# A four-stage network kernel on one core: the finishing of the first attention pinned to its order on VectorE, the norms' shifts gathered into one addition, and pools that wait tile by tile

## The chip, the cores and the metric

The kernel runs on one core of a Trainium2 chip. The metric is the device time of one execution in microseconds. Engines are called PE (TensorE, the matrix unit; PEld is its weight load), DVE (VectorE), ACT (ScalarE), POOL (GpSimd) and SP (SyncE, which issues the transfers). Each engine works through its own list of instructions in order and waits at an instruction until what it needs has been signalled.

## The reference, cut to what matters

All in fp32, T = 1024 tokens of D = 256. Four blocks stand one behind the other, each with a norm before and a norm behind it:

```
x = x + layernorm(attention(layernorm(x)))      # L0: 16 heads of 16, rope, softmax, + its own input
x = x + layernorm(experts_L0(layernorm(x)))     # 8 experts, F = 256, two with low-rank parts
x = x + layernorm(recurrent(layernorm(x)))      # L1: conv over 4 tokens, 16 heads of 128, gated
x = x + layernorm(experts_L1(layernorm(x)))     # 16 experts of 176, the top 4, and a shared one of 352

def layernorm(x):                               # over the 256 values of a token, eps = 1e-5
    m = mean(x); v = var(x)
    return (x - m) / sqrt(v + eps)
```

For the change one property counts: a layernorm does not see a number that is added to all 256 values of a token. The second norm's part in x, written out, is x + acc·rs − mean·rs, where acc is the block's output and rs is 1/sqrt(var + eps). The last term is one number per token.

## The kernel before, in words

The 1024 tokens are 8 tiles of 128 (TT = 8), worked on as four pairs. `x`, `acc` (a block's output) and `hT` (the normed x, channels first, the input of the next block's matmuls) stay in SBUF for the whole run. The four blocks are methods called one after the other: `attention0`, `experts0`, `attention1`, `experts1`. Each opens its own pools of SBUF and PSUM buffers (`a_...`, `b_...`, `c_...`, `d_...`); a block's pools take the memory that the block before it gave back. Weights come by transfers on SP's queue, some groups ahead of use.

**Order.** The program is traced in Python, and a scheduler then puts each engine's instructions in an order of its own choice, from their dependencies and the order of tracing. So two independent instructions of one engine may change places. The engines then run these lists.

**Between two blocks, `turn_over` (L248).** For each pair of tiles: DVE takes the statistics of both `acc` (st, mv: L180, L181), adds eps (ve, L183), POOL raises to the power of −0.5 (rs, L184), DVE works out nb = −mean·rs (L185), adds acc·rs to x (L257), takes statistics of x the same way, ACT writes h = x·rs2 + nb2 (L263), and POOL adds the first norm's nb to x (L267, the shift). Then, some steps later, `turn` (L237) lets PE transpose h (pt, L243) and ACT copy it to hT (L244). The delay is made with the list `todo`: `turn_over` puts two empty steps and the turn on it, and the gate matmuls of the next block pop steps from it (`catch_up`). At the end, `turn_out` (L279) uses the same `scales` and sends x out.

**attention0.** Two halves of 512 queries by four groups of four heads are eight steps. `largest` (L432ff) works ahead: PE scores (L448) by DVE maxima over keys (L453, 256 of them), whose negation goes into an extra row of q and k (L468, then `turned`/`signed`: transposes L406, copies L407). `attend` (L491ff) follows behind it: scores (L517), exponentials on ACT (L546), sums by PE over a block of keys (po, L504), copy of the result (oT, L509). Both are generators that are advanced alternately. When `largest` is through, `attend` takes another branch (`alone`, L526ff), with the exponentials at L535, all four scores first and then the sums of the step before.

The first half of the queries (tiles 0 to 3, two pairs) is finished while the second half is still worked on: `finished_slowly` (L555ff) is a generator, advanced by one step per score pair in `attention0`'s last loop (`next(after, None)`, L696). For each pair it transposes oT (L581), divides by the sums (rec, cx: L586, L587), transposes back (L594, L596), multiplies by w_out (L601), adds the block's own input (acc, L605), and goes through `turn_over_slowly` (L191), the same chain as `turn_over` cut into steps (L201 st, L202 mv, L206 ve, L207 rs, L208 nb, L221 x, L228 h, L233 the shift). The second half (tiles 4 to 7, the third and fourth pair) is finished by `finished(1)`, whose steps go on `todo` and are popped between the first gate matmuls of `experts0`, with `turn_over` at its end.

**The experts.** `experts` (L795ff) runs over groups of experts: gates pg and pu on PE (L765), Silu on ACT (L767), product on DVE (mid, L768), then `down` (po on PE, L783, added to acc by DVE at L791). The gates of groups 0 and 1 come first, and among them the router's logits (pl, L745). `experts1` is `experts` with `join` set. `attention1` projects (px, L1049), does the convolution's taps on DVE (y, L1041), and gates with og (L1265).

Of the kernel before, what the change touches and what calls it, by code (L numbers as in the profile page):

```python
# [15 lines left out]
P = 128  # L16
T = 1024
TT = T // P
# [31 lines left out]
class Net:  # L50
    def __init__(self, ctx, tc, a, out):
# [26 lines left out]
        self.mv0 = self.const.tile([P, TT, 2], F32, name="mv0")  # L78
        self.rs0 = self.const.tile([P, TT], F32, name="rs0")
# [8 lines left out]
        with tc.tile_pool(name="late", bufs=1) as late:  # L88
            self.w_out = late.tile([P, KC, D], F32, name="w_out")
            self.oT = late.tile([P, H * SLOT // P, T], F32, name="oT")  # L90
            with tc.tile_pool(name="awts", bufs=1) as aw:
# [99 lines left out]
    def turn_over_slowly(self, ps, tp, acc):  # L191

        nc = self.nc
# [5 lines left out]
        def stats(mv, i, src):  # L199
            st = self.small.tile([P, 6], F32, tag="st", name="st")  # L200
            nc.vector.bn_stats(st, src)  # L201
            nc.vector.bn_aggr(mv[:, i, :], st)  # L202

        def scale(mv):
            ve, rs, nb = small("ve"), small("rs"), small("nb")
            nc.vector.tensor_scalar(ve, mv[:, :, 1], EPS, None, ALU.add)  # L206
            nc.gpsimd.tensor_tensor(rs, ve, self.nhalf[:, 0:2], ALU.pow)  # L207
            nc.vector.scalar_tensor_tensor(nb, mv[:, :, 0], -1.0, rs, ALU.mult, ALU.mult)  # L208
            return rs, nb

        mv = small("mv", 2)
        for i in range(2):
            acc(i)
            yield
            stats(mv, i, accs[i])
            yield
        rs, nb = scale(mv)
        yield
        mv = small("mv", 2)
        for i, x in enumerate(xs):  # L220
            nc.vector.scalar_tensor_tensor(x, accs[i], rs[:, i : i + 1], x, ALU.mult, ALU.add)  # L221
            yield
            stats(mv, i, x)
            yield
        rs2, nb2 = scale(mv)
        h = self.row.tile([P, 2, D], F32, tag="h2", name="h")
        for i, x in enumerate(xs):
            nc.scalar.activation(  # L228
                h[:, i, :], x, AF.Identity, scale=rs2[:, i : i + 1], bias=nb2[:, i : i + 1]
            )  # L230
            yield
        for i, x in enumerate(xs):
            nc.gpsimd.tensor_scalar(x, x, nb[:, i : i + 1], None, ALU.add)  # L233
        self.turn(ps, h, tp)
        yield

# [11 lines left out]
    def turn_over(self, ps, tts):  # L248

        nc = self.nc
        tp = tts[0] // 2
        xs = self.pair(self.x, tp)
        rs, nb = self.scales(self.pair(self.acc, tp))
        for i, x in enumerate(xs):
            nc.vector.scalar_tensor_tensor(  # L257
                x, self.acc[:, 2 * tp + i, :], rs[:, i : i + 1], x, ALU.mult, ALU.add
            )
        rs2, nb2 = self.scales(xs)  # L260
        h = self.row.tile([P, 2, D], F32, tag="h2", name="h")
        for i, x in enumerate(xs):
            nc.scalar.activation(  # L263
                h[:, i, :], x, AF.Identity, scale=rs2[:, i : i + 1], bias=nb2[:, i : i + 1]
            )
        for i, x in enumerate(xs):
            nc.gpsimd.tensor_scalar(x, x, nb[:, i : i + 1], None, ALU.add)  # L267

        self.todo.extend([None, None, lambda ps: self.turn(ps, h, tp)])
# [107 lines left out]
    def attention0(self):  # L377
# [4 lines left out]
        with ExitStack() as ctx:  # L382
            big = ctx.enter_context(tc.tile_pool(name="a_big", bufs=1))
            qkp = ctx.enter_context(tc.tile_pool(name="a_qk", bufs=2))
            pp = ctx.enter_context(tc.tile_pool(name="a_p", bufs=6))
            ps = ctx.enter_context(tc.tile_pool(name="a_ps", bufs=7, space=PSUM))
            pso = ctx.enter_context(tc.tile_pool(name="a_pso", bufs=1, space=PSUM))
# [167 lines left out]
            def finished_slowly():  # L555
# [3 lines left out]
                for tp in range(QT // 2):  # L559
# [14 lines left out]
                    for _ in self.turn_over_slowly(ps, tp, acc):  # L574
# [3 lines left out]
            def by_token(tt, dst, ps):  # L578
# [7 lines left out]
                nc.vector.reciprocal(rec, pt[:, :, DH : DH + 1])  # L586
                nc.vector.tensor_tensor(dst, pt[:, :, 0:DH], rec.to_broadcast([P, H, DH]), ALU.mult)  # L587
# [11 lines left out]
            def projected(tt, cT, po):  # L599
                for k in range(KC):  # L600
# [4 lines left out]
                nc.vector.scalar_tensor_tensor(  # L605
                    self.acc[:, tt, :], self.x[:, tt, :], self.rs0[:, tt : tt + 1], po,
                    ALU.mult, ALU.add,
# [76 lines left out]
            after = iter(())  # L684
            for n, (qh, g) in enumerate(steps):
                if n == NG:
                    after = finished_slowly()
                then = None
                for inside in attend(qh, g, lambda: pulled == count):
# [3 lines left out]
                    if then:  # L693
                        then()
                        then = None
                    next(after, None)  # L696
            gather(len(sums))
# [97 lines left out]
    def experts(self, ps, tmp, midp, groups, route, weigh, then, join=False):  # L795
# [62 lines left out]
        for g in range(2, len(groups)):  # L858
            tiles = groups[g]()
            for hf in range(2):  # L860
# [21 lines left out]
    def experts0(self):  # L882
        nc, tc, a = self.nc, self.tc, self.a
        with ExitStack() as ctx:
            one = ctx.enter_context(tc.tile_pool(name="b_one", bufs=1))
            midp = ctx.enter_context(tc.tile_pool(name="b_mid", bufs=4))
            tmp = ctx.enter_context(tc.tile_pool(name="b_tmp", bufs=3))
            wp = ctx.enter_context(tc.tile_pool(name="b_w", bufs=4))
            ps = ctx.enter_context(tc.tile_pool(name="b_ps", bufs=8, space=PSUM))
# [83 lines left out]
    def attention1(self):  # L973
# [3 lines left out]
        with ExitStack() as ctx:  # L977
            one = ctx.enter_context(tc.tile_pool(name="c_one", bufs=1))
            sp = ctx.enter_context(tc.tile_pool(name="c_st", bufs=9))
            ps = ctx.enter_context(tc.tile_pool(name="c_ps", bufs=4, space=PSUM))  # L980
            ps2 = ctx.enter_context(tc.tile_pool(name="c_ps2", bufs=2, space=PSUM))
# [458 lines left out]
```

## Time and profile before

| | |
|---|---|
| runs of the kernel | 1282.84, 1286.2, 1287.16 us; median 1286.2 |
| the profiled execution | 1286.36 us, of which its span (first to last instruction) 1284.6 us |
| mean granted clock of TensorE | 0.986 |
| DVE score maxima, L453 | 256 of 685 ns, 163.4 us |
| DVE statistics, L180 | 28 in 11.1 us, 414 ns each |
| POOL power, L184 | 25 in 17.5 us, 701 ns each |
| POOL shift, L267 / L233 | 20 of 968 ns / 4 of 929 ns |
| attention0, experts0, attention1, experts1 begin at | 0, 304.8, 489, 1010 us of the span |

The granted clock is the share of full speed that the chip allowed TensorE; a value of 0.50 means that matmuls take twice as long. In a timeline, a row gives start and duration in us, engine, line and operation, output <- inputs with their sizes, how many instructions were put together (x), and in brackets how long the engine had been idle before it and what ended that.

### The profile page before, as it was taken

To read this page: it belongs to the slowest core of one execution; us is meant where nothing else is said; L and a number is where in the kernel's file an instruction comes from. 1 tells how busy PE (TensorE), PEld (TensorE's weight loads), DVE (VectorE), ACT (ScalarE), POOL (GpSimd) and SP (SyncE) were. 2 spreads that over 40 slices of the span, in tenths; PEclk is the share of its full clock that TensorE was granted. 3 is DMA by queue.
4 is the path that set the end of the run, shared out by engine and by line. 5 is a ranking of instruction groups with operands and counts; after the bars stand their busy time and mean duration, and the time that the engine had idled before them with its cause. 6 is when DMAs were issued, how large, how long until landed. Compare 5 with 4: busy or idle time off the path is not lost. (4 is left out here: it accounts for less than half of the span.)

```text
span 1284.6 us, 15784 instructions
## 1 busy us (share of the span) xinstructions
PE 1217.4 (95%) x6128; PEld 722.3 (56%) x6128; DVE 732.4 (57%) x1656; ACT 495.7 (39%) x912; POOL 149.3 (12%) x137
## 2 busy tenths in 40 slices
PE   7999999989999997899999999999998799999997
PEld 4533333323556564567676667767676346555655
DVE  5876767641542345776777776758675523333334
ACT  4266665655411113544544454453543221111011
POOL 3100001010200022121111112121212400000001
PEclk9999999999999998999999999999999899999999
DMA  6000000000033012002021202020210105523000
GB/s 194 1 1 1 1 1 1 1 1 1 2 129 102 0 42 83 29 33 88 23 103 34 74 33 74 34 74 33 74 41 27 62 1 158 163 82 124 20 25 33
DMA packets 38923, 64.42 MB, mean 50 GB/s; under 512 B 4776, under 2 KB 28552, under 8 KB 38848
## 3 DMA queue, kind: packets, MB, share of 16 engines
q1 hardware_dynamic: 38848, 63.41, 15.4%
q8 instruction: 48, 0.79, 0.3%
q14 instruction: 27, 0.22, 0.1%
HBM read 62.12 MB, written 1.28 MB: 49 GB/s over the span
## 5 line engine op out<-in xcount | busy, mean ns | idle before, releaser
L453 DVE TENSOR_REDUCE pm<-sc 128x1 f32<-128x512 f32 x256 | 163.4, 685 | 66.1 <-PE sc L517 42.9
L768 DVE TENSOR_TENSOR mid<-sg,pu 128x512 f32<-128x512 f32 (+1 forms) x82 | 56.4, 688 | 192.7 <-PE pu L765 163.4
L517 PE MATMUL sc<-qTm,kT 32*128 32x512 f32 x512 | 152.5, 654 | 1.2 <-DVE pm L453 1.2
L767 ACT ACTIVATE sg<-pg 128x512 f32<-128x512 f32 (+1 forms) x82 | 48.9, 596 | 270.5 <-PE pg L765 270.4
L546 ACT ACTIVATE pe<-sc 128x512 f32<-128x512 f32 x216 | 117.8, 595 | 71.0 <-PE sc L517 48.8
L448 PE MATMUL sc<-kT,qT 32*128 32x512 f32 x512 | 139.1, 645 | 1.6 <-ACT qT L407 0.8
L1089 ACT ACTIVATE sn<-pt,shift,rs 128x128 f32<-128x128 f32 x256 | 93.6, 470 | 107.2 <-DVE shift L1085 107.0
L1049 PE MATMUL px<-hT,w_l1a 128*128 128x512 f32 x256 | 124.0, 596 | 4.3 <-issue 3.5
L1041 DVE SCALAR_TENSOR_TENSOR y<-px,cp,y 128x1023 f32<-128x1023 f32 (+5 forms) x102 | 123.2, 1211 | 2.5 <-ACT y L1035 2.5
L791 DVE TENSOR_TENSOR acc<-acc,po 128x512 f32<-128x512 f32 (+1 forms) x61 | 41.1, 674 | 100.1 <-PE po L783 100.1
L765 PE MATMUL pg<-hT,w_l1f 128*128 128x512 f32 (+1 forms) x200 | 97.1, 609 | 0.7 <-ACT hT L244 0.7
L765 PE MATMUL pu<-hT,w_l1f 128*128 128x512 f32 (+1 forms) x200 | 94.7, 596 | 0.0
L783 PE MATMUL po<-w_l1f,mid 128*128 128x256 f32 (+1 forms) x400 | 87.5, 379 | 0.0
L1084 POOL TENSOR_TENSOR rs<-ve,nhalf 128x8 f32<-128x8 f32 x32 | 52.4, 1638 | 299.8 <-DVE ve L1083 245.1
L504 PE MATMUL po<-pe,va 128*32 128x256 f32 (+1 forms) x872 | 80.9, 440 | 4.0 <-ACT oT L509 3.3
L783 PEld LDWEIGHTS po<-w_l1f,mid 128*128 128x128 f32 (+1 forms) x400 | 76.0, 190 | 13.4 <-issue 3.3
L517 PEld LDWEIGHTS sc<-qTm,kT 32*128 32x128 f32 x512 | 49.7, 187 | 53.7 <-issue 41.9
L184 POOL TENSOR_TENSOR rs<-ve,nhalf 128x2 f32<-128x2 f32 (+1 forms) x25 | 17.5, 701 | 464.2 <-DVE ve L183 459.7
L1183 PE MATMUL pg<-hT,w_l1a 128*128 128x512 f32 x128 | 61.9, 609 | 6.9 <-DVE og L1265 5.5
L504 PEld LDWEIGHTS po<-pe,va 128*32 128x32 f32 x872 | 17.8, 108 | 89.0 <-issue 77.5
L765 PEld LDWEIGHTS pu<-hT,w_l1f 128*128 128x128 f32 (+1 forms) x200 | 38.5, 192 | 49.5 <-issue 49.5
L765 PEld LDWEIGHTS pg<-hT,w_l1f 128*128 128x128 f32 (+1 forms) x200 | 38.1, 192 | 44.9 <-issue 43.5
(205 smaller groups left out, 1932.6 us busy)
## 6 DMA issues: line engine op xcount, KB each, us to landing
spread<-rows SPq DMA_DIRECT2D x32, 512.0 KB, 4.5
w<-w SPq DMA_DIRECT2D x16, 512.0 KB, 4.9
w_l1f<-in_e_gT SPq DMA_DIRECT2D x4, 640.0 KB, 4.0
w_l1f<-in_e_uT SPq DMA_DIRECT2D x4, 640.0 KB, 5.3
w_l1f<-in_e_dT SPq DMA_DIRECT2D x4, 640.0 KB, 8.0
w_l0f<-in_e_wg SPq DMA_DIRECT2D x4, 512.0 KB, 5.0
w_l0f<-in_e_wu SPq DMA_DIRECT2D x4, 512.0 KB, 6.5
w_l0f<-in_e_wd SPq DMA_DIRECT2D x4, 512.0 KB, 7.4
```

The lines of the kernel that those rows point to most:

```text
L448: nc.tensor.matmul(sc, raw[r, tt * P : (tt + 1) * P], kT[r, g, half(kh)], start=True, stop=True,)
L453: nc.vector.tensor_reduce(pm[:, tt, 2 * pair + i, kh : kh + 1], sc, AX.X, ALU.max)
L504: nc.tensor.matmul(po[0][rows(j), c], va[:, st, g * G + j, :], pe[j // 2][:, j % 2, c], start=(st == 0), stop=(st == TT - 1 and c.stop == ...
L517: nc.tensor.matmul(sc, kT[rows(j), g, st * P : (st + 1) * P], qm[rows(j), :], start=True, stop=True,)
L546: nc.scalar.activation(pe[pair][:, i, :], sc, AF.Exp, scale=scale)
L765: nc.tensor.matmul(p, w(k), self.hT[:, k, c], start=(k == 0), stop=(k == KC - 1))
L768: nc.vector.tensor_tensor(mid, sg, pu, ALU.mult)
L783: nc.tensor.matmul(po[:, i, :], left[:, at * P : (at + 1) * P], right, start=(n == 0), stop=(n == len(pieces) - 1),)
L1041: nc.vector.scalar_tensor_tensor(y[:, at:hi], px[:, at - j : hi - j], column(cw + 4 * h + 3 - j), y[:, at:hi], ALU.mult, ALU.add,)
L1049: nc.tensor.matmul(px[:, c], w[:, k, hh * DK : (hh + 1) * DK], self.hT[:, k, c], start=(k == 0), stop=(k == KC - 1),)
L1089: nc.scalar.activation(sn[:, n, :], pts[n // 4][:, n % 4, :], AF.Identity, scale=rs[:, n : n + 1], bias=shift[:, n : n + 1],)
L1183: nc.tensor.matmul(pg, wg[:, k, hh * DK : (hh + 1) * DK], self.hT[:, k, c], start=(k == 0), stop=(k == KC - 1),)
```

## The change

Three things are altered.

1. `turning` takes the place of `turn_over_slowly` and of the body of `turn_over`. Its DVE instructions, and `rec`, `cx` and `acc` of attention0, are *pinned*: the scheduler keeps each of them on DVE behind all that was pinned before it. The second statistics are interleaved (x, st, mv of the first tile, then of the second). The steps of the finishing are advanced twice per score pair once `largest` is through, and the last transposes of q and k are put off by two steps (`late`). `turn_over` takes 12 pieces of `turning` at once and leaves the turn on `todo`, as before.
2. The POOL additions of nb to x (L233, L267) are gone. Means and rs of the first norms are kept for all eight tiles and the three blocks (`mvs`, `rss`), and `shifted`, called at the fourth group of `experts1` (g = 3), works out the sum of the three shifts on POOL and adds it to x with eight ACT instructions. nb is now worked out for the second norm only.
3. All pools of the four blocks are opened with `reuse_waits="tile"`: a buffer waits for the last users of the very bytes that it takes over, where before it waited for all users of the pool that had the memory.

The diff, cut to its core (the pools' lines all alike):

```diff
-        with tc.tile_pool(name="late", bufs=1) as late:
+        with tc.tile_pool(name="late", reuse_waits="tile", bufs=1) as late:
...
         self.nhalf = self.const.tile([P, TT], F32, name="nhalf")
         nc.gpsimd.memset(self.nhalf, -0.5)
         self.mv0 = self.const.tile([P, TT, 2], F32, name="mv0")
+        self.mvs = self.const.tile([P, 3, TT, 2], F32, name="mvs")
+        self.rss = self.const.tile([P, 3, TT], F32, name="rss")
+        self.norms = [0] * (TT // 2)
         self.rs0 = self.const.tile([P, TT], F32, name="rs0")
...
     def pair(self, v, tp):
         return [v[:, 2 * tp + i, :] for i in range(2)]
-    def turn_over_slowly(self, ps, tp, acc):
-        nc = self.nc
+    def pinned(self, ins):
+        return self.tc.keep_in_program_order(ins)
+    def turning(self, ps, tp, acc=None):
+        nc, pinned = self.nc, self.pinned
         xs, accs = self.pair(self.x, tp), self.pair(self.acc, tp)
         def small(tag, *shape):
...
         def stats(mv, i, src):
             st = self.small.tile([P, 6], F32, tag="st", name="st")
-            nc.vector.bn_stats(st, src)
-            nc.vector.bn_aggr(mv[:, i, :], st)
-        def scale(mv):
-            ve, rs, nb = small("ve"), small("rs"), small("nb")
-            nc.vector.tensor_scalar(ve, mv[:, :, 1], EPS, None, ALU.add)
+            pinned(nc.vector.bn_stats(st, src))
+            pinned(nc.vector.bn_aggr(mv[:, i, :], st))
+        def scale(mv, rs):
+            ve = small("ve")
+            pinned(nc.vector.tensor_scalar(ve, mv[:, :, 1], EPS, None, ALU.add))
             nc.gpsimd.tensor_tensor(rs, ve, self.nhalf[:, 0:2], ALU.pow)
-            nc.vector.scalar_tensor_tensor(nb, mv[:, :, 0], -1.0, rs, ALU.mult, ALU.mult)
-            return rs, nb
-        mv = small("mv", 2)
+        n = self.norms[tp]
+        self.norms[tp] += 1
+        mv, rs = (v[:, n, 2 * tp : 2 * tp + 2] for v in (self.mvs, self.rss))
         for i in range(2):
-            acc(i)
+            if acc is not None:
+                acc(i)
             yield
             stats(mv, i, accs[i])
             yield
-        rs, nb = scale(mv)
+        scale(mv, rs)
         yield
-        mv = small("mv", 2)
+        mv2, rs2 = small("mv", 2), small("rs")
         for i, x in enumerate(xs):
-            nc.vector.scalar_tensor_tensor(x, accs[i], rs[:, i : i + 1], x, ALU.mult, ALU.add)
+            pinned(nc.vector.scalar_tensor_tensor(x, accs[i], rs[:, i : i + 1], x, ALU.mult, ALU.add))
             yield
-            stats(mv, i, x)
+            stats(mv2, i, x)
             yield
-        rs2, nb2 = scale(mv)
+        scale(mv2, rs2)
+        yield
+        nb = small("nb")
+        pinned(nc.vector.scalar_tensor_tensor(nb, mv2[:, :, 0], -1.0, rs2, ALU.mult, ALU.mult))
+        yield
         h = self.row.tile([P, 2, D], F32, tag="h2", name="h")
         for i, x in enumerate(xs):
             nc.scalar.activation(
-                h[:, i, :], x, AF.Identity, scale=rs2[:, i : i + 1], bias=nb2[:, i : i + 1]
+                h[:, i, :], x, AF.Identity, scale=rs2[:, i : i + 1], bias=nb[:, i : i + 1]
             )
-            yield
-        for i, x in enumerate(xs):
-            nc.gpsimd.tensor_scalar(x, x, nb[:, i : i + 1], None, ALU.add)
+        ps = (yield) or ps
         self.turn(ps, h, tp)
         yield
+    PIECES = 12
     def turn(self, ps, h, tp):
...
     def turn_over(self, ps, tts):
-        nc = self.nc
-        tp = tts[0] // 2
-        xs = self.pair(self.x, tp)
-        rs, nb = self.scales(self.pair(self.acc, tp))
-        for i, x in enumerate(xs):
-            nc.vector.scalar_tensor_tensor(
-                x, self.acc[:, 2 * tp + i, :], rs[:, i : i + 1], x, ALU.mult, ALU.add
-            )
-        rs2, nb2 = self.scales(xs)
-        h = self.row.tile([P, 2, D], F32, tag="h2", name="h")
-        for i, x in enumerate(xs):
-            nc.scalar.activation(
-                h[:, i, :], x, AF.Identity, scale=rs2[:, i : i + 1], bias=nb2[:, i : i + 1]
-            )
-        for i, x in enumerate(xs):
-            nc.gpsimd.tensor_scalar(x, x, nb[:, i : i + 1], None, ALU.add)
-        self.todo.extend([None, None, lambda ps: self.turn(ps, h, tp)])
+        t = self.turning(ps, tts[0] // 2)
+        for _ in range(self.PIECES):
+            next(t)
+        self.todo.extend([None, None, lambda ps: t.send(ps)])
+    def shifted(self):
+        nc = self.nc
+        lost = self.small.tile([P, 3, TT], F32, tag="lost", bufs=1, name="lost")
+        shift = self.small.tile([P, TT], F32, tag="shift", bufs=1, name="shift")
+        nc.gpsimd.tensor_tensor(lost, self.mvs[:, :, :, 0], self.rss, ALU.mult)
+        nc.gpsimd.tensor_tensor(shift, lost[:, 0, :], lost[:, 1, :], ALU.add)
+        nc.gpsimd.tensor_tensor(shift, shift, lost[:, 2, :], ALU.add)
+        nc.gpsimd.tensor_scalar(shift, shift, -1.0, None, ALU.mult)
+        for tt in range(TT):
+            x = self.x[:, tt, :]
+            self.pinned(nc.scalar.activation(x, x, AF.Identity, bias=shift[:, tt : tt + 1]))
     def catch_up(self, ps, n):
...
                         po = ps.tile([P, D], F32, tag="b1", name="po")
                         projected(2 * tp + i, cT[:, :, i, :], po)
-                    for _ in self.turn_over_slowly(ps, tp, acc):
+                    for _ in self.turning(ps, tp, acc):
                         yield
                         yield
...
                         oT[:, g, tt * P : (tt + 1) * P], self.ident,
                     )
                 rec = self.small.tile([P, H, 1], F32, tag="rec", name="rec")
-                nc.vector.reciprocal(rec, pt[:, :, DH : DH + 1])
-                nc.vector.tensor_tensor(dst, pt[:, :, 0:DH], rec.to_broadcast([P, H, DH]), ALU.mult)
+                self.pinned(nc.vector.reciprocal(rec, pt[:, :, DH : DH + 1]))
+                self.pinned(
+                    nc.vector.tensor_tensor(dst, pt[:, :, 0:DH], rec.to_broadcast([P, H, DH]), ALU.mult)
+                )
             def by_channel(cx, ps):
                 cx = cx.rearrange("p i h c -> p i (h c)")
...
                         po, cT[:, k, :], self.w_out[:, k, :], start=(k == 0), stop=(k == KC - 1)
                     )
-                nc.vector.scalar_tensor_tensor(
-                    self.acc[:, tt, :], self.x[:, tt, :], self.rs0[:, tt : tt + 1], po,
-                    ALU.mult, ALU.add,
+                self.pinned(
+                    nc.vector.scalar_tensor_tensor(
+                        self.acc[:, tt, :], self.x[:, tt, :], self.rs0[:, tt : tt + 1], po,
+                        ALU.mult, ALU.add,
+                    )
                 )
             def finished(qh):
...
                 then = pull()
                 if then:
                     then()
-            after = iter(())
+            after, then, late = iter(()), None, 2
             for n, (qh, g) in enumerate(steps):
                 if n == NG:
                     after = finished_slowly()
-                then = None
                 for inside in attend(qh, g, lambda: pulled == count):
                     if inside:
                         then = pull()
                         continue
-                    if then:
+                    if pulled == count and late > 0:
+                        late -= 1
+                    elif then:
                         then()
                         then = None
                     next(after, None)
+                    if pulled == count:
+                        next(after, None)
             gather(len(sums))
             for _ in after:
                 pass
...
         behind = []
         for g in range(2, len(groups)):
             tiles = groups[g]()
+            if join and g == 3:
+                self.shifted()
             for hf in range(2):
                 half = start(g, tiles, hf)
                 if join and g >= len(groups) - 2 and (g, hf) != (len(groups) - 2, 0):
```

## The prediction

> **What bounds the kernel now.** I read the page's first part, then the idle time ahead of TensorE (PE), then the timeline at each idle place, then the granted clock around it.
>
> ```profile
> span 1284.6 us, 15784 instructions
> PE 1217.4 (95%) x6128; PEld 722.3 (56%) x6128; DVE 732.4 (57%) x1656; ACT 495.7 (39%) x912; POOL 149.3 (12%) x137
> PEclk9999999999999998999999999999999899999999
> ```
>
> PE is busy 1217.4 of 1284.6 us, so everything else can give back at most 67 us. DVE (57%) and POOL (12%) count only where PE stands still for them. PE's order is almost untouched by the change (it issues the same matmuls; the order differs only while attention0 finishes and experts0 starts), so the forecast is a sum over the few places where PE stands. They all lie where one stage is finished by norms and the next begins.
>
> ```profile
> 219.81 0.16 DVE L208 SCALAR_TENSOR_TENSOR nb<-mv,rs 128x2 f32<-128x2 f32 x1 [0.81 <-POOL rs L207]
> 220.01 1.09 ACT L228 ACTIVATE h<-x,nb,rs 128x256 f32<-128x256 f32 x2 [3.27 <-DVE nb L208]
> 220.63 1.12 PE L517 MATMUL sc<-qTm,kT 32*128 32x512 f32 x2 [1.21 <-DVE pm L453]
> 220.71 1.83 POOL L233 TENSOR_SCALAR x<-x,nb 128x256 f32<-128x256 f32 x2 [0.93 <-ACT h L228]
> ...
> 225.82 1.94 PE L504 MATMUL po<-pe,va 128*32 128x512 f32 x8
> ...
> 229.30 0.64 PE L504 MATMUL po<-pe,va 128*32 128x256 f32 x8
> ```
>
> That is the timeline where the first pair of attention0 is finished. The finishing's twelve small DVE operations came bunched between 213.9 and 220.0, the score maxima (L453) came late, PE waited 1.21 us, and then the same eight sums (L504) that take 0.64 us elsewhere took 1.94. The stretches of the clock say why:
>
> ```profile
> 218.61:222.02 3.41, 2.20 (x16) 1.03 (x14) 2.56 (x7) 2.01 (x5) 2.01 (x3) 1.00 0.00 0
> 222.02:228.85 6.83, 6.83 (x29) 2.59 (x26) 3.11 (x5) 3.19 (x7) 0.52 (x1) 0.50 0.00 0
> ...
> 476.00:479.70 3.70, 1.23 (x7) 0.53 (x5) 2.75 (x10) 0.68 (x2) 1.30 (x2) 1.00 0.00 0
> 479.70:486.50 6.80, 6.74 (x33) 5.79 (x34) 2.44 (x7) 1.46 (x3) 2.66 (x3) 1.00 0.00 0
> ```
>
> Columns: window, PE, PEld, DVE, ACT and POOL busy, granted clock. After some stalls PE runs at 0.50 for 6.83 us, which costs half of that, 3.4 us, if PE has work throughout.
>
> **The change, part by part.** Five places; times are of the profiled execution.
>
> *First pair of attention0 (215 to 230), DVE's order pinned, two sums of scores between any two pieces.* A steady group (eight score matmuls and eight sums) takes PE 1.64 to 1.66 us, by the starts of the groups away from any stall, and DVE 1.29 (two maxima of 0.65). From 214.93 to 229.87 PE did five groups, 14.94 us, against 5 x 1.64 = 8.2: 6.8 lost. Pinned, one piece (at most x 0.48 or st 0.43 + mv 0.18) falls to every two groups: 4 x 0.65 + 0.61 = 3.2 us of DVE against 3.3 of PE. It just fits, so no bunch, no stall, no slow clock. The ends are 0 (maxima late anyhow) and 6.8; I take **-6**, near the upper end, since nothing else feeds the bunch.
>
> *Second pair, tail of attention0 (268 to 305).* PE's 1.43-us wait at 270.3 for the turn of the last q and k goes (that turn is now put off by two steps).
>
> ```profile
> 283.69 0.60 ACT L228 ACTIVATE h<-x,nb,rs 128x256 f32<-128x256 f32 x1 [2.07 <-DVE nb L208]
> 284.20 0.56 ACT L509 COPY oT<-po 128x512 f32<-128x512 f32 x1
> 284.82 1.94 PE L504 MATMUL po<-pe,va 128*32 128x512 f32 x8 [3.27 <-ACT oT L509]
> ```
>
> Before, ACT waited for nb, and the copy oT behind it held PE 3.3 us; 6.83 us of half clock followed. In the new order the two h still stand ahead of that copy on ACT. nb is worked out at 280.9 (from the projection's start, now 274.0, by the old chain of 6.2 us plus 0.45 for the norm's new interleaving), so a stall like the old one stays, but from then on ACT has 28 exponentials of 0.52 us and ends near 299.7; the first gate matmul starts near 301 with no slow clock, 303.5 with it, against 304.76. Gain 1.3 to 3.9, taken **-2.2**.
>
> *Start of experts0 (321 to 340), third and fourth pair.* This is what the change costs.
>
> ```profile
> 330.56 1.09 ACT L263 ACTIVATE h<-x,nb,rs 128x256 f32<-128x256 f32 x2 [3.36 <-DVE nb L185]
> ...
> 334.77 1.09 ACT L263 ACTIVATE h<-x,nb,rs 128x256 f32<-128x256 f32 x2 [2.64 <-DVE nb L185]
> 335.42 0.93 PE L243 MATMUL pt<-ident,h 128*128 128x128 f32 x4
> ...
> 339.62 3.63 PE L745 MATMUL pl<-wr,hT 128*128 128x8 f32 x32
> ```
>
> Before, the scheduler mixed the two pairs: the sums acc of all four tiles stood ahead of the third pair's x, and the fourth pair's nb came 4.2 us after the third's. Pinned, the fourth pair's acc (tile 6) stands behind the third pair's nb on DVE (331.3). Behind it wait PE's projection of tile 7 (same PSUM bank; PE gets there near 330, so 1.3 to 1.9 us idle), then acc 7, and the whole chain: st, idr's copy (0.66), st, mid (0.69), ve, pow 0.73, x, st, x, st, mid, ve, pow, nb = 9.3 us from 331.8, nb near 341, first h near 340.5 to 341.7. PE reaches the fourth pair's transposes near 337 and waits 3.7. The router's logits, 339.62 before, come near 344.5 to 345.5: **+5**. Ends: 0 (DVE fills the waits for pow with mids, and all pairs come 1 us earlier) and +8 with half clock. A stall of 3.3 us (284.82, above) and one of 3.5 (498.88, below) each stood beside 6.83 us at 0.50, one of 2.47 at 477 did not; so I add 0.6 x 3.4 = **+2**.
>
> *experts0 to attention1, attention1 to experts1 (470 to 512, 991 to 1015).* All turns now go x, st, mv, x, st, mv, which costs 0.45 us against x, x, st, st, mv, mv (each mv waits for its st). Where PE already waits for h, this is paid: 2.47 us at 477 becomes about 3, +0.5, or +3.9 if the clock falls there; I take **+0.5** and **+1** for a third of a chance.
>
> ```profile
> 498.88 1.18 PE L243 MATMUL pt<-ident,h 128*128 128x128 f32 x4 [3.48 <-ACT h L263]
> ...
> 1001.73 0.93 POOL L267 TENSOR_SCALAR x<-x,nb 128x256 f32<-128x256 f32 x1 [0.93 <-ACT h L263]
> 1002.63 0.73 POOL L184 TENSOR_TENSOR rs<-ve,nhalf 128x2 f32<-128x2 f32 x1
> 1008.25 1.18 PE L243 MATMUL pt<-ident,h 128*128 128x128 f32 x4 [5.63 <-ACT h L263]
> ```
>
> Here POOL's x (0.93) does stand ahead of a pow that the chain waits for; its removal gives 0.75 to 0.9, the interleaving and one convolution tap (0.7) that now precedes the norm's last ve take it back: **0** at 499. At 1002 the first pair's nb comes about 2 us later and the last h about 0.6: **+0.6** (-0.5 to +1.5).
>
> *The shifts.* 24 POOL adds of 0.93 to 0.97 us (22.9 us) go; POOL is 12% busy and, but for the two places above, nobody waits for them: 0. The new ones are four small POOL operations and eight ACT operations 128x256, like h (0.55): 4.4 us in experts1, where ACT has one Silu of 0.6 us per 3.44 us of PE. PE has eight banks ahead of it: 0, at worst 1. They would have to delay a Silu by more than those banks hold to be seen. If that cover were gone, it would be the 4.4 us. The pools' finer waits change one place I can find: the first px (489.27, idle 1.76) need not wait for the last acc, 1.8 us earlier, but the next transposes wait for h at 498.9 either way: 0.
>
> Sum: -6 - 2.2 + 5 + 2 + 0.5 + 1 + 0.6 = **+0.9**. From the profiled 1286.36 (span 1284.6 and 1.8 around it; the median 1286.2 is the same) that gives **1287**. A difference under 0.3% (3.9 us) can't be told from none.
>
> [...]
>
> **Rivals.**
>
> *Faster, about 1279* (1275 to 1282.4). The fourth pair's norm isn't late: the new stalls at 330 and 337 are short because PE's start moves 2 us ahead and DVE's mids fall elsewhere; then -6 - 2.2 + 1 = -7. For it: DVE has idle time around 329 to 336. Against: acc 6 is behind nb in the built order.
>
> *Slower, about 1293* (1290.2 to 1297). One mechanism: the fourth pair's acc behind the third's nb at the start of experts0, stall 3.7 + 1.9, the half clock in full after it (+3.4), and no gain from the tail: -6 + 5.6 + 3.4 + 0.5 + 3.4 (the same at 477) = +7. It decides as soon as the first pair gains less than the fourth loses. For it: 3.5 us idle at 495 did bring the half clock.
>
> *Nothing of it works*: DVE's pinned pieces still bunch (3.2 of 3.3 us leaves no slack), first pair's slow clock stays: -2 + 8 = 1292; this lies in the same range as the slower rival.
>
> **How the numbers follow.** Forecast 0.41 (own range 1282.5 to 1290.1), faster 0.29, slower 0.25, nothing works 0.05. The range 1277.5 to 1295 reaches into both sides and leaves out the ends of each. Faster by over 0.3% 0.29, within 0.41, slower 0.30.
>
> **What would show it.** Right: no PE row of over 1 us of idle and no clock of 0.50 between 214 and 232; the transposes of the fourth pair with an idle of 3 us or more for h, and logits 4 us or more after the first gate plus 34.9 (before: 339.62 - 304.76); px 2 us earlier with the same end. Wrong: a half clock at 222 still there; logits within 36 us of the first gate; the tail's stall gone (a copy oT ahead of h on ACT); a Silu of experts1's group 3 with PE idle behind it.

## The result, and the profile after

The changed kernel takes 1285.95 us (median of 12 runs, 1284.49 to 1290.56) against 1285.98 (12 runs, 1282.84 to 1287.38): ratio 1.0005, interval 0.9995 to 1.0015. No difference can be told. The profiled execution took 1284.57 us with a span of 1282.5, 1.8 less than that of before.

That is not because nothing happened. The first lines of the page after, for the sum, and the clock of the stretch where the first pair of attention0 is finished (window, PE, PEld, DVE, ACT and POOL busy, granted clock):

```profile
span 1282.5 us, 15734 instructions
PE 1215.0 (95%) x6128; PEld 722.3 (56%) x6128; DVE 733.5 (57%) x1644; ACT 498.6 (39%) x920; POOL 126.9 (10%) x117
```

```profile
215.20:222.02 6.82, 6.82 (x56) 2.30 (x48) 5.39 (x11) 4.63 (x9) 0.71 (x1) 1.00 0.00 0
222.02:228.85 6.83, 6.83 (x68) 2.50 (x64) 5.86 (x11) 4.34 (x8) 0.00 (x0) 1.00 0.01 2
```

PE does 68 matmuls from 222.02 to 228.85 where it did 29, at full clock. Then, in the timeline of the kernel after, the tail of attention0, and the first gate of experts0:

```profile
274.60 0.16 DVE L239 SCALAR_TENSOR_TENSOR nb<-mv,rs 128x2 f32<-128x2 f32 x1 [0.81 <-POOL rs L216]
274.80 1.09 ACT L243 ACTIVATE h<-x,nb,rs 128x256 f32<-128x256 f32 x2 [2.42 <-DVE nb L239]
...
276.42 1.12 PE L529 MATMUL sc<-qTm,kT 32*128 32x512 f32 x2 [1.86 <-ACT pe L547]
277.70 0.60 ACT L521 COPY oT<-po 128x512 f32<-128x512 f32 x1
...
296.41 1.99 PE L784 MATMUL pg<-hT,w_l0f 128*128 128x512 f32 x4
```

ACT still waits 2.42 us for nb with its two h ahead of the exponentials, and PE waits for these. And the start of experts0:

```profile
321.92 0.16 DVE L239 SCALAR_TENSOR_TENSOR nb<-mv,rs 128x2 f32<-128x2 f32 x1 [0.81 <-POOL rs L216]
322.00 0.47 DVE L620 SCALAR_TENSOR_TENSOR acc<-x,rs,po 128x256 f32<-128x256 f32 x1
...
322.53 1.13 PE L615 MATMUL po<-w_out,cT 128*128 128x256 f32 x4 [0.90 <-DVE acc L620]
...
331.08 1.09 ACT L243 ACTIVATE h<-x,nb,rs 128x256 f32<-128x256 f32 x2 [3.71 <-DVE nb L239]
331.74 0.44 PE L258 MATMUL pt<-ident,h 128*128 128x128 f32 x2 [3.35 <-ACT h L243]
...
337.36 3.63 PE L764 MATMUL pl<-wr,hT 128*128 128x8 f32 x32
```

The fourth pair's acc runs right behind the third pair's nb (322.00 after 321.92), the projection of tile 7 waits for it (0.90), and 9 us later the transposes wait 3.35 us for its h. The logits stand 40.95 us behind the first gate (296.41). In the kernel before it was 34.86, from its logits at 339.62 and its first gate:

```profile
304.76 1.98 PE L765 MATMUL pg<-hT,w_l0f 128*128 128x512 f32 x4 [0.68 <-ACT hT L244]
```

The later turns, in the timeline of the same kernel: the first projection px no longer waits, the last pair's transposes wait longer, and at the end of attention1 two pairs are waited for instead of one.

```profile
477.56 0.93 PE L258 MATMUL pt<-ident,h 128*128 128x128 f32 x4 [2.63 <-ACT h L243]
...
485.24 1.88 PE L1070 MATMUL px<-hT,w_l1a 128*128 128x512 f32 x4
...
496.30 1.18 PE L258 MATMUL pt<-ident,h 128*128 128x128 f32 x4 [4.76 <-ACT h L243]
...
1001.16 1.18 PE L258 MATMUL pt<-ident,h 128*128 128x128 f32 x4 [3.70 <-ACT h L243]
...
1006.15 1.18 PE L258 MATMUL pt<-ident,h 128*128 128x128 f32 x4 [3.81 <-ACT h L243]
```

Two rows of the kernel before for the same places, the second pair's h at the end of experts0 and the first px:

```profile
479.67 0.93 PE L243 MATMUL pt<-ident,h 128*128 128x128 f32 x4 [2.47 <-ACT h L263]
...
489.27 1.96 PE L1049 MATMUL px<-hT,w_l1a 128*128 128x512 f32 x4 [1.76 <-issue]
```

Cut at the starts of the same matmuls, PE's time falls into these stretches (us, from the traces; the columns on the right belong to the experiments below):

| stretch | before | after | e1 | e2 | e6 | e4 | e7 | e8 | e5 | e10 |
|---|---|---|---|---|---|---|---|---|---|---|
| A: 1st to 701st sum of attention0 (first pair) | 181.61 | 175.69 | 175.69 | 181.54 | 175.69 | 175.69 | 175.69 | 175.69 | 175.69 | 175.69 |
| T: to the first gate of experts0 | 54.75 | 53.44 | 53.59 | 53.32 | 53.41 | 54.23 | 53.40 | 53.57 | 53.59 | 49.45 |
| B: to the logits | 34.86 | 40.95 | 34.53 | 34.53 | 39.37 | 39.27 | 34.53 | 35.78 | 34.53 | 34.53 |
| M: to the first px | 149.64 | 147.88 | 147.04 | 148.74 | 149.59 | 151.48 | 151.26 | 149.57 | 147.04 | 148.72 |
| C: to the last pair's transposes | 9.61 | 11.06 | 9.75 | 9.75 | 11.07 | 9.12 | 11.06 | 9.87 | 9.75 | 9.75 |
| D: last head of attention1 to the first gate of experts1 | 14.08 | 14.50 | 12.97 | 12.97 | 14.51 | 14.57 | 14.50 | 13.60 | 12.97 | 12.97 |
| to the last matmul | 266.81 | 266.82 | 266.71 | 266.64 | 266.62 | 266.94 | 267.14 | 266.29 | 266.81 | 266.50 |

From before to after: A -5.9, T -1.3, B +6.1, M -1.8, C +1.4, D +0.4, the rest 0 (from the end of C to the start of D it is 497.1 us before and 497.2 after); ahead of the first sum of attention0 1.1 us less, in a part of the program that the change doesn't touch (over all profiles that stretch is 67.3 to 69.5 us long). attention0 gains 7.2 us and the start of experts0 gives 6.1 of them back.

### The profile page after: what moved, and what is told of

Read it like the earlier page. It is cut to its first block, busy times and chain, and to the rows that moved or that the text cites. A ratio compares the mean times of both kernels' runs of the same rounds, so it can differ in the third digit from the quotient of the medians.

```text
span 1282.5 us, 15734 instructions
## 1 busy us (share of the span) xinstructions
PE 1215.0 (95%) x6128; PEld 722.3 (56%) x6128; DVE 733.5 (57%) x1644; ACT 498.6 (39%) x920; POOL 126.9 (10%) x117
## 5 line engine op out<-in xcount | busy, mean ns | idle before, releaser
L460 PE MATMUL sc<-kT,qT 32*128 32x512 f32 x512 | 136.3, 638 | 1.6 <-ACT qT L419 0.8
L784 PE MATMUL pg<-hT,w_l0f 128*128 128x512 f32 x128 | 61.7, 604 | 0.0
```

The costliest lines, as they stand in the source:

```text
L460: nc.tensor.matmul(sc, raw[r, tt * P : (tt + 1) * P], kT[r, g, half(kh)], start=True, stop=True,)
L784: nc.tensor.matmul(p, w(k), self.hT[:, k, c], start=(k == 0), stop=(k == KC - 1))
```

## The experiments

My theory: the pin spreads the first pair's finishing and is worth 6 us there; the same pin, applied to the second half, is what costs 6 us at the start of experts0. The rival: the extra delays in attention0 do the good, and the loss is something else that comes with it. All ratios are to the kernel before, run on the same chip.

**e1, pinned in the first half of attention0 alone.**

```diff
-        return self.tc.keep_in_program_order(ins)
+        return self.tc.keep_in_program_order(ins) if self.pin else ins
...
+            self.pin = False
             self.todo.extend(finished(1))
```

> Pinned only while the first half of attention0 is finished; the second half and all later turns are left to the scheduler. Theory (the pin gains some 7 us in attention0 and loses 6 at the start of experts0 and 2 at 1002): the first gate stays near 296.4 as in the changed kernel, the logits come 35 us behind it instead of 41, and the first gate of experts1 another 2 us nearer: about 1278 us, ratio to before 0.993 to 0.995. Rival (the loss at the start of experts0 comes from the shorter attention0, whose weights or second half are not ready, not from the pin): logits 40 us or more behind the first gate, about 1285.

Measured: 1276.4 us (1272.87 to 1278.92), ratio 0.992 (0.9906 to 0.9934), 1.6 us below what I had expected. A and T are as in the changed kernel, B is 34.53; M, C and D are shorter by 0.8, 1.3 and 1.5. The timeline of e1 at the place of the loss:

```profile
316.90 0.48 DVE L621 SCALAR_TENSOR_TENSOR acc<-x,rs,po 128x256 f32<-128x256 f32 x1
...
322.15 0.16 DVE L240 SCALAR_TENSOR_TENSOR nb<-mv,rs 128x2 f32<-128x2 f32 x1
322.23 0.16 DVE L216 TENSOR_SCALAR ve<-mvs 128x2 f32<-128x2 f32 x1
...
323.20 0.88 DVE L233 SCALAR_TENSOR_TENSOR x<-acc,rss,x 128x256 f32<-128x256 f32 x2 [0.81 <-POOL rss L217]
...
326.17 1.09 ACT L244 ACTIVATE h<-x,nb,rs 128x256 f32<-128x256 f32 x2 [2.25 <-DVE nb L240]
327.44 0.60 PE L259 MATMUL pt<-ident,h 128*128 128x128 f32 x4
```

The last of the four acc is at 316.90, 5 us ahead of the third pair's nb. The fourth pair's first statistics run between the third pair's second ones (320.48 to 321.49), and its ve follows the third pair's nb at once; its h is 3.83 us behind the third pair's (322.34), where it was 8.96 (331.08 less 322.12). PE does not wait. So the loss of B comes from the pin of the second half, and the rival falls.

**e2, nothing pinned on DVE.**

```diff
-        return self.tc.keep_in_program_order(ins)
+        return ins
```

> Nothing is pinned on VectorE; the delayed last turn of q and k, the double steps, the gathered shifts and the finer waits stay. Theory (the pin is what spreads the first pair's finishing): the small operations bunch again near 214 to 220, with a stall of 1 us or more and 6.8 us of half clock; 5 to 6 us of attention0's gain are lost, and the 6 us at the start of experts0 are not paid: about 1284 to 1286. Rival (the extra steps spread it, the pin does not matter there): no slow clock near 222, first gate near 296.4 and logits 35 behind it, about 1278.

Measured: 1282.16 us (1279.56 to 1283.34), ratio 0.9963 (0.995 to 0.9976), 2 us under what the theory gave and 4 above the rival. A is 181.54, as before. The timeline of e2, and the clock of the same stretch:

```profile
219.43 0.16 DVE L239 SCALAR_TENSOR_TENSOR nb<-mv,rs 128x2 f32<-128x2 f32 x1 [0.81 <-POOL rs L216]
219.63 1.09 ACT L243 ACTIVATE h<-x,nb,rs 128x256 f32<-128x256 f32 x2 [3.20 <-DVE nb L239]
...
225.44 1.94 PE L516 MATMUL po<-pe,va 128*32 128x512 f32 x8
```

```profile
215.20:221.60 6.40, 5.19 (x37) 1.79 (x30) 5.41 (x14) 2.59 (x7) 0.74 (x2) 1.00 0.00 0
221.60:228.40 6.80, 6.80 (x29) 2.59 (x26) 3.16 (x5) 3.23 (x7) 0.00 (x0) 0.50 0.00 0
```

The bunch, the short wait and the half clock are back, with the delays still in. The pin is what spreads the first pair. What e2 gains against before (T -1.4, M -0.9, D -1.1) needs no pin.

**e6, all pinned, but all four acc ahead of both norms.**

```diff
-                    self.turn_over(ps, [2 * tp, 2 * tp + 1])
+                    if tp == tps[-1]:
+                        for tq in tps:
+                            self.turn_over(ps, [2 * tq, 2 * tq + 1])
```

> Still all pinned, but the sums acc of all four tiles of the second half are traced, and so pinned, ahead of both pairs' norms (the third pair's turn_over is called only once the fourth pair is projected). Theory (what was lost at the start of experts0 is the fourth pair's acc behind the third pair's nb): the 0.9-us wait at the projection of tile 7 goes, the 3.4-us wait of the fourth pair's transposes shrinks to 1 to 2.5 us, since its norm still stands wholly behind the third pair's; logits 37 to 39 us behind the first gate, 2 to 4 us faster than the changed kernel, about 1283. Rival (the interleaved norm itself is what is late): the wait stays at 3 us or more.

Measured: 1285.94 us (1285.23 to 1287.84), ratio 0.9999 (0.9991 to 1.0008): no gain in time, so the size was missed. The waits at tile 7 and for the fourth pair's h are gone (0.16 us is left), but with all four acc ahead of it the third pair's norm is late now. The timeline of e6, the third pair's nb and transposes and then the fourth's:

```profile
326.22 0.16 DVE L239 SCALAR_TENSOR_TENSOR nb<-mv,rs 128x2 f32<-128x2 f32 x1 [0.81 <-POOL rs L216]
...
327.07 0.44 PE L258 MATMUL pt<-ident,h 128*128 128x128 f32 x2 [2.54 <-ACT h L243]
...
332.17 0.16 DVE L239 SCALAR_TENSOR_TENSOR nb<-mv,rs 128x2 f32<-128x2 f32 x1 [0.81 <-POOL rs L216]
...
333.01 0.44 PE L258 MATMUL pt<-ident,h 128*128 128x128 f32 x2 [0.16 <-ACT h L243]
```

The fourth pair's nb comes 34.6 us behind the first gate (297.57), as late as in the changed kernel (34.5); in e1 it is 29.2. So B fell by 1.6 only, to 39.37, of which 3.4 us of half clock make 1.7 as in the changed kernel, and the profile's M is 1.7 longer by another 3.4 us (see below). The place of the acc alone is not what makes the fourth pair late. The pinned norms, one wholly behind the other, end as late in either order, and the wait only moved to the third pair: the mechanism was missed too, and the rival was nearer to it.

**e4, without the finer waits of the pools.** All `reuse_waits="tile"` are taken out.

> The changed kernel without the finer waits of the pools. Theory: only the first projection of attention1 changes, 1.8 us later, and the transposes for the last pair's h take it back: 0 to +1.9 us, 1286 to 1288. Rival (the finer waits carry part of the gain of attention0 or of experts0): +3 us or more, with the difference before 480.

Measured: 1288.17 us (1286.76 to 1290.7), ratio 1.0012 (1.0003 to 1.002), 2.2 above the changed kernel; with each set against the kernel before beside it (1286.41 and 1285.98) it is 1.8, inside what the theory gave, though the two intervals overlap. px is 1.9 us later (M, beside 3.4 us of half clock), and the wait for the last pair shorter by 1.8 (2.99 against 4.76), so C gives 1.9 back (9.12 against 11.06). Nothing before 480 speaks for the rival but 0.8 us in T.

**e7, free only in the second half of attention0; all other turns pinned.**

```diff
         nc, pinned = self.nc, self.pinned        # self.pinned as in e1
+        if self.norms[tp] > 0:
+            pinned = self.tc.keep_in_program_order
```

> Pinned for the first half of attention0 and for the turns behind experts0 and attention1, free only for the second half of attention0 (its quotients, sums acc and norms). Theory (the pin's loss is three separate losses: 6 us at the start of experts0, 0.9 us in the wait at 477, 3 us in the turn at 1002): the logits come 34.5 us behind the first gate, but the wait near 470 stays 2.8 us and the first gate of experts1 comes 10.9 us behind the last gated product as in the changed kernel, not 7.8: about 1280 us, 3 to 4 above the kernel that is pinned in the first half alone. [...]

Measured: 1280.66 us (1279.75 to 1284.02), ratio 0.9963 (0.995 to 0.9977): 4.3 above e1, or 5.2 with each set against the kernel before beside it. B is 34.53; the waits of the later turns are those of the changed kernel. Against e1 they cost 0.85 at the transposes near 477 (M, beside 3.4 for half clock behind the logits), 1.3 in C and 1.5 in D (14.50 less 12.97), where I had expected 3 and no cost in C: without the pin PE waits 1.3 us for og instead (989.07 in e1).

**e8, e1 with the shifts on POOL again.**

```diff
+        lost = small("lost")
+        pinned(nc.vector.scalar_tensor_tensor(lost, mv[:, :, 0], -1.0, rs, ALU.mult, ALU.mult))
+        for i, x in enumerate(xs):
+            nc.gpsimd.tensor_scalar(x, x, lost[:, i : i + 1], None, ALU.add)
...
-            if join and g == 3:
-                self.shifted()
```

> Pinned in the first half of attention0 alone, and the shifts are added pair by pair on GpSimd again, as before, with the small product for them on VectorE. Theory of the prediction (nobody waits for these additions but at two places, where they stand ahead of a pow): 0.8 us each at 492 and 1002, so 1 to 2 us above the kernel without them, 1277 to 1279. Rival (the additions and the second small product are a good part of the gain behind attention0, at 477, 490 and 1002): +3 to +4 us, about 1280.

Measured: 1278.6 us (1278.2 to 1281.7), ratio 0.9949 (0.9936 to 0.9962), 2.2 above e1, or 3.1 with each set against the kernel before beside it. By stretches: B +1.25, the wait near 477 +0.83, C +0.1, D +0.6, 2.8 in all, nearer to the rival than to the theory. The interval of e8 overlaps that of e1's repetition below (0.9916 to 0.9946), so the size rests on the stretches. The timeline of e8 shows how:

```profile
322.90 0.93 POOL L250 TENSOR_SCALAR x<-x,lost 128x256 f32<-128x256 f32 x1 [0.93 <-ACT h L244]
...
323.80 0.73 POOL L217 TENSOR_TENSOR rss<-ve,nhalf 128x2 f32<-128x2 f32 x1
...
324.52 0.93 POOL L250 TENSOR_SCALAR x<-x,lost 128x256 f32<-128x256 f32 x1
324.56 1.10 DVE L233 SCALAR_TENSOR_TENSOR x<-acc,rss,x 128x256 f32<-128x256 f32 x2 [1.58 <-POOL rss L217]
```

The third pair's addition (322.90) stands ahead of the fourth pair's pow, so DVE's two x (324.56) start 27.7 us behind the first gate, against 26.4 in e1 (323.20), and they take 1.10 us, 0.88 in e1. So an addition delays the next pair's norm where the pairs follow close.

**e5, e1 with one step per score pair and no delay of the last turn of q and k.**

```diff
-            after, then, late = iter(()), None, 2
+            after, then, late = iter(()), None, 0
...
-                    if pulled == count:
-                        next(after, None)
```

> Pinned in the first half of attention0 alone, with one step of the finishing per score pair to the end and without the delay of the last turn of q and k. Theory: the first pair is as good as with them (no slow clock near 222), but the wait of 1.4 us ahead of the last turn of q and k comes back and the second pair's h are 4 us later in the tail; some 1 to 3 us lost at the first gate: 1277 to 1280. Rival (the delays do most of the work in attention0): +5 us and more.

Measured: 1279.63 us (1275.2 to 1281.33), ratio 0.9948 (0.9932 to 0.9963), 3.2 above e1 in the median, though the two profiled executions have the same stretches (T 53.59 in both). One profile of each can't say which holds, so both kernels were measured again on one chip:

> One step of the finishing per score pair and no delay of the last turn, pinned in the first half alone, again, since its median stood 3.2 us above the kernel with both while its profile showed the same stretches. If the edit costs nothing: within 1 us of that kernel on this chip. If it costs something that the one profile missed: 2 to 4 us above it.

> Pinned in the first half of attention0 alone, again, as the measure for the run before it: 1274 to 1278 us.

Measured: e5 again 1280.1 us (1279.83 to 1281.4), ratio 0.9958 (0.9946 to 0.997); e1 again 1276.32 us (1274.87 to 1279.44), ratio 0.9931 (0.9916 to 0.9946). The edit does cost 3 to 4 us, and this time the profile has it: T is 56.29 against 53.41. In the timeline of e5 again the wait ahead of the last turn of q and k is back (1.06 us by its row), and h comes so late that the first gate waits for the copy to hT:

```profile
265.30 0.66 PE L419 MATMUL pt<-ident,qk 128*128 128x128 f32 x4 [1.06 <-DVE qk L481]
...
280.96 1.09 ACT L244 ACTIVATE h<-x,nb,rs 128x256 f32<-128x256 f32 x2 [2.43 <-DVE nb L240]
282.59 2.07 PE L530 MATMUL sc<-qTm,kT 32*128 32x512 f32 x2 [1.88 <-ACT pe L548]
...
299.77 1.98 PE L784 MATMUL pg<-hT,w_l0f 128*128 128x512 f32 x4 [0.68 <-ACT hT L260]
```

The rest is the clock: 6.8 us at half behind the wait at 280, none in e5's first profile, 3.4 in e1. So the two steps and the delay are worth 3 to 4 us in most executions, the pin 6.

**e10, e1 with the tail's exponentials and h kept in order on ACT.**

```diff
-                            nc.scalar.activation(pe[pair][:, i, :], sc, AF.Exp, scale=scale)
+                            self.pinned(nc.scalar.activation(pe[pair][:, i, :], sc, AF.Exp, scale=scale))
...
-            nc.scalar.activation(
+            self.pinned(nc.scalar.activation(
                 h[:, i, :], x, AF.Identity, scale=rs2[:, i : i + 1], bias=nb[:, i : i + 1]
-            )
+            ))
```

> Pinned in the first half of attention0 alone, and on ScalarE the second pair's two h and the exponentials of the tail are kept in the order of tracing too, which puts h 12 exponentials later (6 us), behind the copy oT. Theory (the two waits of 2.4 and 1.4 us at 274 to 278 come from h ahead of exponentials and copy on ScalarE, waiting 2.4 us for nb): both go, with the 3.4 us of half clock behind them; ScalarE loses 0.5 us between h and the copy to hT; first gate 3 to 5 us earlier, 1272 to 1274. Rival (the tail is bound by ScalarE's 36 exponentials, the waits only move): within 1 us, 1276.

Measured: 1272.55 us (1268.94 to 1273.57), ratio 0.9889 (0.9874 to 0.9905), the fastest. T is 49.45, 4.1 less than in e1. Its timeline:

```profile
274.44 0.62 ACT L525 COPY oT<-po 128x512 f32<-128x512 f32 x1
274.80 0.16 DVE L240 SCALAR_TENSOR_TENSOR nb<-mv,rs 128x2 f32<-128x2 f32 x1 [0.81 <-POOL rs L217]
...
275.11 1.07 PE L520 MATMUL po<-pe,va 128*32 128x512 f32 x8 [0.35 <-ACT oT L525]
...
281.32 1.11 ACT L247 ACTIVATE h<-x,nb,rs 128x256 f32<-128x256 f32 x2
...
293.56 0.70 PE L789 MATMUL pg<-hT,w_l0f 128*128 128x512 f32 x1
```

Run again beside e1 it took 1271.16 us (1268.43 to 1273.4), ratio 0.988 (0.9862 to 0.9898), with the same T of 49.45.

The copy oT no longer stands behind h, nb is 6 us old when h is worked out, and PE waits 0.35 us where it waited 1.87 and 0.81 in e1. The 3.4 us of half clock that followed there (from 278.49) are gone too.

**e12, e10 with the router's matmuls of experts0 64 wide** (56 columns of zeros in the weights, whose results nobody reads), for a question that the profiles raised: in nine of the thirteen with narrow logits PE falls to half clock at the end of the 32 logits matmuls, which are 8 wide, or within them. Does it still do so when they are wide?

```diff
-            wr = one.tile([P, KC, E0], F32, name="wr")
+            wr = one.tile([P, KC, 64], F32, name="wr")
+            nc.gpsimd.memset(wr, 0.0)
...
-        pl = self.logits(ps, wr, E0)
+        pl = self.logits(ps, wr, 64)[:, :, 0:E0]
```

> The last kernel (ScalarE's tail in order), with the router's matmuls of experts0 64 wide instead of 8: 56 columns of zeros are added to the weights, the results of which nobody reads. [...]

> The same kernel with 8 columns again, beside it on this chip: 1270 to 1274 us. [...]

Measured: e12 1269.95 us (1268.82 to 1273.55), ratio 0.9882 (0.9865 to 0.9899), against 0.988 (0.9862 to 0.9898) of e10 beside it. The 32 matmuls 64 wide took 3.68 us, against 3.74 of those 8 wide in e10's repetition, and behind them e12's profile has no half clock (1.00 from 326.9 to 333.8; M 147.03 against 148.72), but the times can't be told apart, and one profile isn't enough: four with 8 columns had none either. So it stays open whether the width matters.

## Why the prediction was right, and where its terms were not

The forecast was no change, by gains in attention0 that the start of experts0 takes back, and that is what the stretches show. That the sum is so near has some luck in it: the tail gave 0.9 us less than forecast and the start of experts0 took 0.9 less, and two of the terms were chances of the clock. Term by term:

- **First pair, -6:** A measured -5.9. Shown by e2, which loses it again without the pin. One reading behind it was wrong: the sums that took 1.94 us at 225.82 are 512 columns wide, those of 0.64 us 256. At full clock eight wide ones take 1.06 (at 220.20 in the kernel after), so the half clock cost 0.9 us there, not 1.3. The loss of 6.8 (6.7 by its own numbers) was taken from the starts of the groups and does not rest on it.
- **Tail, -2.2 (1.3 to 3.9):** T -1.3, the lower end. The wait for the last turn of q and k, which went, had been 1.06 us (271.70 in the kernel before), not 1.43. The wait for nb stayed, as said, and e10 shows what was left there: 4.1 us.
- **Start of experts0, +5 and +2 for the clock:** B +6.1. The wait at tile 7 is 0.90 (1.3 to 1.9 said) and that for the fourth pair's h 3.35 (3.7 said). Half clock follows (332.6 to 336.0), 3.4 us of it and not 6.8, so 1.7 us; 4.4 are the waits. e1 shows that the pin at this place costs them. The forecast laid the lateness to the fourth pair's acc behind the third pair's nb; e6 shows that this is not enough of a cause, since with all acc ahead the fourth pair's nb is as late (34.6 us behind the first gate, against 34.5). What e1 lets happen, and the pin forbids, is that the two norms fill each other's waits.
- **477 and 499, +1.5 and 0:** this term was mis-sized. The wait near 477 grew by 0.16 us (2.47 to 2.63), not 0.5, and no half clock fell there. Two things cancel, which e7 and e8 part: the pin costs 0.85, the additions on POOL that are gone give 0.83. px came 1.9 us earlier (1.8 said), and C took back 1.4 of it, not all.
- **1002, +0.6:** D +0.4, again out of two that cancel: +1.5 for the pin (e7 against e1) and -1.1 for the rest of the change (e2 against before), of which the additions are 0.6 (e8).
- **The shifts, 0:** the step that failed is "but for the two places above, nobody waits for them". e8 measures 2.2 us in the median and 2.8 in the stretches, 1.25 of it where the third and the fourth pair follow each other in experts0, a place that I did not count, since PE did not wait there before. What the additions cost in the kernel before, with its own order of DVE, no run shows apart: B of e2, without pin and without additions, is only 0.33 below that of before. The eight additions on ACT cost nothing as said:

```profile
L281 ACT ACTIVATE x<-x,shift 128x256 f32<-128x256 f32 x8 | 3.3, 495 | 0.0
```

They take 3.3 us together (4.4 said), and the stretch from the first gate of experts1 to the end is 266.82 against 266.81.

The faster rival had the right size for the wrong kernel: it is e1, where the fourth norm isn't late. The stalls of the slower rival are there (3.35 and 0.90 us, where it had 3.7 and 1.9), but the tail kept its gain and the clock fell for 3.4 us, not 6.8, and not at 477.

## What to carry to other kernels

Pinning an order to that of the program pays where small operations must be spread among long ones (here 5.9 us), and costs where two independent chains with waits could fill each other's gaps (here 4.4 us, and 1.7 by the clock): pin the one place, not the helper that all places share. When a change moves nothing, cut the traces at the same matmuls and look for the parts that cancel; here undoing the costly half was worth 0.7 to 0.8%, and the waits that were left in the tail another 0.3 to 0.5%. An operation on an engine that is 12% busy is free only as long as nothing queues behind it on that engine at the few places that matter: those on POOL cost 2.8 us in e8, by the stretches.

## What the runs showed of the hardware

The clock of PE fell without any wait of PE. In nine of the thirteen profiles with narrow logits a stretch of half clock of 3.4 or 6.8 us begins at the end of the 32 logits matmuls of experts0 or within them. The clock of e10 around its logits (328.10 to 331.84), and of e7 around its own (332.15 to 336.27):

```profile
327.50:331.20 3.70, 3.70 (x31) 3.29 (x29) 0.69 (x1) 1.04 (x1) 0.00 (x0) 1.00 0.01 2
331.20:334.60 3.40, 3.40 (x9) 1.85 (x9) 1.62 (x7) 0.26 (x1) 0.00 (x0) 0.54 0.00 0
```

```profile
325.00:335.00 10.00, 10.00 (x48) 6.12 (x46) 3.10 (x9) 4.41 (x7) 0.69 (x1) 1.00 0.01 2
335.00:341.80 6.80, 6.80 (x15) 3.62 (x15) 1.62 (x7) 2.08 (x3) 0.00 (x0) 0.51 0.00 0
```

PE shows busy throughout (3.70 and 3.40 us in e10, 10.00 and 6.80 in e7). With the half clock M can be counted to 0.05 us: 147.04 (e1: no half clock, a wait of 1.79 near 477) plus half of the slow time, plus 0.85 for the longer wait there, plus 1.9 where px waits. e10: 147.04 + 1.7; e7: + 3.4 + 0.85; e4: + 1.7 + 0.85 + 1.9. In the logits of experts1, 16 wide, the same is seen: in the kernel before they end at 1044.06, and 3.41 us of half clock begin at 1044.63; in the kernel after 1041.98 and 1042.56.

The length of a wait does not tell by itself whether the clock falls. In the kernel after, waits of PE of 3.35, 4.76, and 3.70 with 3.81 us had 3.41, 6.83 and 10.24 us of half clock beside them, and 2.63 none; but one of only 1.86 (276.42) had 3.41 us too, and at the logits PE does not wait. Nor does its busy time just ahead: in the kernel before PE was busy 2.20 of the 3.41 us ahead of the half clock at 222.02, and all of the 3.41 us ahead of that at 1044.63. The stretches of that trace up to 1045 begin at 222.02, 283.46, 498.50, 1007.08 and 1044.63; the gaps between these starts, 61.44, 215.04, 508.58 and 37.55 us, are 18, 63, 149 and 11 times 3.413 us. What draws the half clock at the narrow logits no run shows; the wide form, with none behind it, has one profile.

What it costs is seen at the gate matmuls of experts1 (pg, 512 wide): in both kernels they start 0.854 us apart at 0.50, 0.429 at 1.00.

Much of the runs' spread goes with the clock: the changed kernel took 1284.5 us at a mean granted clock of 0.988, 1288.7 at 0.984 and 1290.6 at 0.981; e10 and its repetition 1268.4 at 0.994 and 1273.6 at 0.989. A clock lower by 0.005 is 6.4 us of PE's work over 1270, where the times differ by 5.1. It is not all of it: e1 again took 1274.87 us at 0.989 and 1278.75 at 0.990.

And where DVE's two x start just behind the start of an addition on POOL, with which they share no data, the first takes longer: 0.63 us in the kernel before, at all six such places, against 0.45 to 0.48 at the others. In e8 the two take 1.10 us together at such places (324.56 and 469.78), 0.88 at another without (319.06). The second takes 0.47 us in the kernel before, also where an addition runs beside it throughout (332.11), so it is not shown that running beside an addition is what slows the first.
